# Two transformer layers on one core: longer transfer times in the list run, and a row's output projection and SwiGLU four attention steps later

## The chip, the cores and the metric

The kernel runs on one core of a Trainium2 chip. The metric is the device time of one execution in microseconds (us), given as the median of several runs.

## The reference

The input is eight sequences ("rows" below) of 512 tokens with 256 channels, and a condition vector of 64 numbers for each row. Two layers follow one another, all in float32:

```
# layer 0: conditioned norm, GELU-gated feed-forward, quantised down projection, residual
scale = cond @ norm_w.T + 1.0
h = x * (scale * rsqrt(mean(x * x) + 1e-6))
val, gate = split(h @ up_w.T, 2)              # 256 -> 2 x 1024
h = val * gelu(gate)
x = x + act_quant(h) @ weight_quant(down_w).T # 8-bit steps per token, weights of -1, 0, 1
# layer 1: adaptive norm, attention, adaptive norm, SwiGLU
n = gamma(cond) * rmsnorm(x) + beta(cond)
attn = softmax(0.25 * q k^T) v                # 16 heads of 16 channels, 512 x 512 scores each
x = x + alpha(cond) * (attn @ W_o.T)
n = gamma2(cond) * rmsnorm(x) + beta2(cond)
x = x + alpha2(cond) * ((silu(n @ gate_w.T) * (n @ hidden_w.T)) @ out_w.T + out_b)
```

## The kernel before

The kernel does not write its instructions in program order. Each piece of work is recorded with `op(engine, cost, fn, reads, writes, at, ...)`: its engine, an assumed duration, what it reads and writes, and a due time `at`. Then `Plan.order` runs a list schedule over all recorded pieces: on each engine it takes the piece with the earliest due time that could start now, by assumed durations and assumed latencies, and the instructions are issued in the order so found. Buffers are slots of named pools (`pools`), and the list run also decides which slot a value gets. On the chip each engine then executes its list strictly in that order and waits on semaphores. Nothing of the assumed times is on the chip; they decide the order alone.

Three things shape the list run beside costs and due times. `LATENCY` is the time from the end of a piece to when another engine may use it: 0.1 to 0.25 us for compute engines and 2.5 us for `SP`, which issues nearly all transfers. `lag` adds to that for single pieces. `SEEDS` holds one number for each 12 us of assumed time; a number other than 0 shifts due times of some lines in that stretch and changes how PE pieces of one kind are grouped (`nudge`).

The work falls into stages. Layer 0 of rows 0 to 5 comes first (up to about 210 us): `up_tile` makes a tile of 128 tokens with full-array matmuls (line 763), GELU on ACT (770), the gate product on DVE (797), the quantisation, a transposing transfer on SP (`qtrans`, line 840), and `down` (848). Layer 0 of rows 6 and 7 is mixed into the attention of row 0 as filler.

The attention of a row has 4 units of 4 heads (two halves `c` of the channels, two groups `j` in each), 32 units in all, and 4 steps a unit, 128 steps in all, which the list run places `STEP` = 5.8 us apart. For a unit, `load_unit` fetches q, k and kd (differences of k) from DRAM into `aq` and `ad` (line 976); `maxima` (1021) multiplies q and k to find the largest score of each query, six steps ahead (`LEAD`), which DVE reads off (1030); `shift` brings the maxima back as a row vector through a transposing transfer (1064); `scores` (1003, 1006) computes the shifted scores, ACT takes the exponential (1037), and `products` (1082) multiplies with v. There are three buffers for q and two for k. A k buffer is free again after the first step of `scores` of its unit (line 1006 with k), and the first `maxima` of the next unit but one need the new k about two steps later.

Between the steps PE does filler, mostly in 32-column quarters of the array (`quarters`, line 428): the projection of the next row (`project`, whose results `send` writes to DRAM as `hld` and `hdd`, line 890, eight transfers for k and its differences and four for q of each half), and the output projection and SwiGLU of the row before (`project_out`, `swiglu`). `gather` brings a unit's products out: to `zd` in DRAM (1096), back as sums `rec` and heads `zn` (1112, 1115), the reciprocal to `rd` (1118) and back (1123), and POOL multiplies (1127). `project_out` reads that, DVE multiplies by the condition's alpha (`gate`, 1164), and POOL adds to x (1173). `swiglu` starts with a norm (squares on DVE 601, root on POOL 611 and 613, scaling on DVE 619), POOL adds the output bias times alpha (`obs`, 1188), and then come gate and hidden products, the down product, `gate_and_add` again, and the store.

`load_gates(b)` fetches the alphas of row b into one of two `als` buffers (1134, on SP), and POOL multiplies them with the bias (1139). The buffer is that of row b - 2, and is free when the last `gate` (1164) of that row's `swiglu` is done. POOL's list is executed in order, so what stands behind line 1139 waits for that transfer too.

The loop over steps places a row's output projection and SwiGLU by due time:

```
        if w >= 1 and k == 0:
            d = s + 2.5 + 0.8 * (w - 1)
            project_out(w - 1, fill(d))
            swiglu(w - 1, fill(d), d + 2.5, fill, PACE)
```

Of the kernel before, what the change touches and what calls it, by code (L numbers as in the profile page):

```python
# [51 lines left out]
DH = 16  # L52
# [22 lines left out]
class Plan:  # L75
# [19 lines left out]
    LOOK = 12.0  # L95
    SPREAD = 1.5
    SEEDS = [
        0, 113879, 0, 0, 0, 0, 0, 0, 0, 691441, 257665, 0, 717272, 393272, 0, 554462, 316701, 670129, 416392,
        721209, 474305, 0, 537810, 342162, 308204, 358595, 0, 701966, 797240, 775750, 239774, 554473, 917419,
        473329, 441941, 90862, 278546, 410234, 995329, 846992, 293684, 929624, 744201, 712144, 709987, 445396,  # L100
        898520, 758230, 941880, 341522, 204408, 437273, 600013, 665815, 561999, 815879, 930, 731008, 247712,
        207304, 666590, 130391, 5386, 637252, 0, 357611, 936297, 455395, 157162, 681884, 543189, 851877,
        58582, 407043, 728554, 327633, 571631, 96113, 784247, 475861, 58555, 909861,
    ]

    def __init__(self, pools):
# [2 lines left out]
    def op(self, engine, cost, fn, reads=(), writes=(), at=0.0, also=(), mode="full", gate=None, mark=None, loads=False, lag=0.0):  # L109
        o = Op()  # L110
        o.loads, o.lag = loads, lag
        o.gate, o.mark = gate, mark
        o.engine, o.cost, o.fn, o.at, o.n, o.mode = engine, cost, fn, at, len(self.ops), mode
        deps = set()
        for v in reads:
            deps.update(v.writers)
            v.readers.append(o.n)
        for v in writes:
            deps.update(v.writers)
            deps.update(v.readers)  # L120
            v.writers, v.readers = [o.n], []
        deps.discard(o.n)
        o.deps = deps
        o.vals = list(dict.fromkeys([*writes, *reads, *also]))
        for v in o.vals:
            v.touch += 1
        o.users, o.waiting, o.ready, o.end = [], len(deps), 0.0, None
        for d in deps:
            self.ops[d].users.append(o.n)
        self.ops.append(o)  # L130
        return o
# [178 lines left out]
def dma(kb):  # L310
    return max(0.6, kb / 250)
# [3 lines left out]
def two_layers(ctx: ExitStack, tc: tile.TileContext, x, cond_t, cond_w, up_t, down_t, qkvo_t, gh_t, out_t, out_b, out):  # L315
# [53 lines left out]
    def mem(v):  # L369

        kind, i = v.slot[0]
        arena = {"b": banks, "4": a4, "2": a2, "q": aq, "d": ad, "al": als, "ob": obs}[kind]
        n = len(v.slot)
        return arena[:, i, :] if n == 1 else arena[:, i : i + n, :]
# [69 lines left out]
    def load(name, dst, src, at, cost=0.6, gate=None, queue=sp):  # L444
        op("SP" if queue is sp else "ACT", cost, lambda: queue.dma_start(out=dst(), in_=src), writes=[V[name]], at=at, gate=gate)

    load("ct", lambda: ct, cond_t, -89, queue=se)
    load("nw", lambda: mem(V["nw"])[:C, :D], cond_w[:, :D], -95)
    load_x(0, -96, n=2)
    wup, up_v = {}, up_t.rearrange("(c p) f -> p c f", p=P)  # L450

# [302 lines left out]
    def up_tile(b, t, ht, at, late=False):  # L754
# [94 lines left out]
                    mem(py)[:, :D], i[:, f * P : (f + 1) * P], w, start=f == 0, stop=f == NF - 1  # L849
                )  # L850

        op("SP", 1.5, qtrans, reads=[q], writes=[qt], at=a8, lag=1.0)
        op("PE", 0.9, down, reads=[qt, *wq], writes=[py], at=a14, gate=after(a14) if late else None,
           mode="columns" if late else "full")
        op(
# [19 lines left out]
    def project(b, at, places):  # L875
# [7 lines left out]
        def send(s, hl, m, a):  # L883

            for k in range(4):
                l = k % 2 if s else k // 2
                o = hdd[b % 2, c] if s == 2 else hld[b % 2, c, s]
                op(
                    "SP", dma(m / 2),
                    lambda l=l, k=k, o=o: sp.dma_start(out=o[:, k], in_=mem(hl)[:, l * m : (l + 1) * m]),  # L890
                    reads=[hl], writes=[vhld[b % 2][c][s][k]], at=a, lag=1.5,
                )

        for c in range(NC):
# [72 lines left out]
    def load_unit(m, at):  # L967


        b, c, j = units[m]  # L970
        for s, name in enumerate(("q", "k", "kd")):
            w = val[name, m] = Val(name)

            def fetch(s=s, w=w):
                i = hdd[b % 2, c] if s == 2 else hld[b % 2, c, s]
                sp.dma_start(
                    out=mem(w).bitcast(F32), in_=i[4 * j : 4 * j + 4].rearrange("(p e) k d s -> (e k d) p s", e=2)
                )

            op("SP", dma(384 if s == 2 else 512), fetch, reads=vhld[b % 2][c][s], writes=[w], at=at + 5 * (s == 2),  # L980
               lag=1.0)

    def tile_of(m, name, p, e):

# [56 lines left out]
    def shift(m):  # L1041


        k = m % 2
        at = when(4 * m - LEAD + 3 + HALF)

        def column(i):
            return thirds[:, k].rearrange("p t (e r) -> p e t r", e=2)[:, :, :, :8].rearrange(
                "p e t (i l) -> p i e t l", l=4
            )[:, :, :, :, i]  # L1050

        def whole(v):
            return v[:, k].rearrange("p (i e) t -> p i e t", e=2)

        def split():
            ve.tensor_copy(column(0), whole(tops))
            ve.tensor_tensor(whole(rest), whole(tops), column(0), op=ALU.subtract)
            ve.tensor_copy(column(1), whole(rest))
            ve.tensor_tensor(column(2), whole(rest), column(1), op=ALU.subtract)

        op("DVE", 0.95, split, reads=[vtop[k]], writes=[vthird[k]], at=at)

        def send():
            sp.dma_start_transpose(
                shifts[:, k, :].rearrange("r (t q) -> r t q", t=NT), thirds[:, k].rearrange("q t r -> q (t r)")
            )

        op("SP", 1.2, send, reads=[vthird[k]], writes=[vshift[k]], at=at, lag=1.0)

    def weigh(s):  # L1070
        n, kc = divmod(s, 4)
# [17 lines left out]
    def gather(n):  # L1089

        b, c, j = units[n]
        pa, zc = val["pa", n], Val("zc")
        at = when(4 * n + 5.1)
        op("ACT", act(512), lambda: se.activation(mem(zc), mem(pa), AF.Identity), reads=[pa], writes=[zc], at=at)
        d = vzd[b % 2][c]
        op("SP", dma(256), lambda: sp.dma_start(out=zd[b % 2, c, j], in_=mem(zc)), reads=[zc], writes=[d], at=at)
        if j == 0:
            return
        if c == 0:
            val["zn", b] = Val("zn")  # L1100
        zn, s = val["zn", b], Val("s")

        def z_of():
            return mem(zn)[:, c * S : (c + 1) * S]

        def blocks():
            return zd[b % 2, c].rearrange("j (i r) s -> (j i) r s", r=32)

        r, vr = rec[:, c, :], vrec[c]
        op(  # L1110
            "SP", 0.6,
            lambda: sp.dma_start(out=r, in_=blocks()[:, DH, :].rearrange("h (k s) -> h k s", k=DH)),
            reads=[d], writes=[vr], at=at,
        )
        op("SP", dma(256), lambda: sp.dma_start(out=z_of(), in_=blocks()[:, :DH, :]), reads=[d], writes=[zn], at=at)
        op("DVE", 0.35, lambda: ve.reciprocal(r, r), writes=[vr], at=at)
        op(
            "SP", 0.6, lambda: sp.dma_start(out=rd[b % 2, c].rearrange("h (k s) -> h k s", k=DH), in_=r),
            reads=[vr], writes=[vrd[c]], at=at,
        )  # L1120
        op(
            "SP", dma(256),
            lambda: sp.dma_start(out=mem(s), in_=rd[b % 2, c].unsqueeze(1).to_broadcast([8, DH, S])),
            reads=[vrd[c]], writes=[s], at=at,
        )
        op(
            "POOL", pool(512), lambda: gp.tensor_tensor(z_of(), z_of(), mem(s), op=ALU.mult),  # L1127
            reads=[s], writes=[zn], at=at + 2,
        )
# [149 lines left out]
    for s in range(-LEAD, 4 * len(units)):  # L1279
        w, k = divmod(s, 16)  # L1280
        m, qc = divmod(s + LEAD + 4, 4)
        if qc == 0 and 2 <= m < len(units):
            load_unit(m, when(s))
        for p in range(2):
            half_step(s, p)
        if (s + LEAD) % 4 == 3 and s + LEAD < 4 * len(units):
            shift((s + LEAD) // 4)
        if s >= 1:
            weigh(s - 1)
            if s % 4 == 0:  # L1290
                gather(s // 4 - 1)
        if w >= 0 and k == 0 and w + 1 < B:
            project(w + 1, fill(s - 1), [fill(s + d) for d in (1, 3, 6, 9, 11, 13)])
        if s == 0:
            for n in range(LATE * NT):
                b, t = B - LATE + n // NT, n % NT
                up_tile(b, t, hts[b], lambda i, n=n: fill((0.5 + 2.05 * n if n < LATE * NT - 1 else 17.5) + i), True)
        if w >= 0 and k == 8:
            load_gates(w)
        if w >= 1 and k == 0:  # L1300
            d = s + 2.5 + 0.8 * (w - 1)
            project_out(w - 1, fill(d))
            swiglu(w - 1, fill(d), d + 2.5, fill, PACE)
    weigh(4 * len(units) - 1)
# [46 lines left out]
```

## Time and profile before

| | us |
|---|---|
| median of 3 runs | 1064.88 (1060.07 to 1069.7) |
| profiled execution | 1064.92 |
| its span, first to last instruction | 1063.1 |
| PE busy in the span | 1031.8 (97%) |
| DVE busy | 636.9 (60%) |
| ACT busy | 525.9 (49%) |
| POOL busy | 219.6 (21%) |
| mean granted PE clock | 0.995 |

The profile is of one execution. An engine is busy when it executes; what it waited for before an instruction is told in brackets as "idle time and releaser". "SPq" is the queue of SP, which only issues transfers. PE's share says that it is nearly always at work; a clock below 1 says that PE was slowed for a part of the stretch.

### The profile page before, as it was taken

The numbers are of one execution on the slowest core, as the hardware profiler recorded it, in microseconds if no ns is written. First come the engines' busy times: TensorE is split into PE (matmuls) and PEld (weight loads), VectorE is DVE, ScalarE is ACT, GpSimd is POOL, SyncE is SP. The second block draws the span as 40 slices with busy tenths as digits, with TensorE's granted clock in tenths as the row PEclk, the third lists the DMA queues.
The fourth block names the chain that finished last, engine by engine and source line by source line (L and its number), as shares of the span: only waits on it lengthen the run. The fifth ranks groups of instructions, "written<-read, shape, count | busy, mean of one in ns | idle before, by whom it ended". The sixth has DMA issues, their size and how long they took to land.

```text
span 1063.1 us, 21750 instructions
## 1 busy us (share of the span) xinstructions
PE 1031.8 (97%) x9016; PEld 425.4 (40%) x9016; DVE 636.9 (60%) x1060; ACT 525.9 (49%) x722; POOL 219.6 (21%) x214
## 2 busy tenths in 40 slices
PE   7999989999999999999999999999899999999998
PEld 3445445433333333433443343334333433342446
DVE  3765546878776765576558547665676465663131
ACT  3434424357677645455546553564556355546221
POOL 2100100001000331043123212321331132223342
PEclk9999999999999999999999999999999999999999
DMA  6344683227564754475256537634752745321100
GB/s 197 88 106 104 187 209 75 50 55 199 147 161 95 201 157 134 138 221 186 83 163 205 144 116 219 190 99 134 218 158 85 198 149 147 126 80 47 33 21 20
DMA packets 131235, 142.07 MB, mean 134 GB/s; under 512 B 60472, under 2 KB 87288, under 8 KB 131136
## 3 DMA queue, kind: packets, MB, share of 16 engines
q1 hardware_dynamic: 130912, 140.42, 47.3%
q8 instruction: 70, 1.15, 0.4%
q10 hardware_dynamic: 224, 0.26, 0.1%
q14 instruction: 29, 0.24, 0.1%
HBM read 69.08 MB, written 59.00 MB: 120 GB/s over the span
## 4 chain that ended last, share of the span: by engine, by line
PE 84%; DMA 9%; DVE 2%; SPq 1%; ACT 1%; POOL 1%; issue 1%; DVEq 0%; ACTq 0%; POOLq 0%
PE banks L428 38%; PE banks L763 15%; PE banks L1082 9%; PE banks L1021 6%; PE banks L1006 6%; DMA aq<-hld 3%; PE banks L1201 3%; DMA a<-a 2%; PE banks L848 2%; PE banks L1003 1%; PE banks L1242 1%; PE banks L434 1%; DMA rd<-rec 1%; SPq L890 1%; DMA a<-rd 1%; DVE tops L1030 1%
## 5 line engine op out<-in xcount | busy, mean ns | idle before, releaser
L1030 DVE TENSOR_REDUCE tops<-banks 128x2 f32<-128x1024 f32 x256 | 308.5, 1220 | 137.7 <-PE banks L1021 135.2
L1037 ACT ACTIVATE a<-banks 128x1024 f32<-128x1024 f32 x256 | 252.5, 1024 | 128.3 <-PE banks L1006 102.8
L428 PE MATMUL banks<-a,gh 128*32 128x512 f32 x1792 | 206.1, 594 | 0.0
L763 PE MATMUL banks<-a,a 128*128 128x512 f32 x384 | 174.8, 603 | 0.6 <-ACT a L726 0.6
L1082 PE MATMUL banks<-a,vts 128*32 128x512 f32 x1024 | 135.2, 606 | 0.1
L1229 POOL TENSOR_TENSOR a<-a 128x512 f32<-128x512 f32 x64 | 81.8, 1279 | 233.8 <-ACT a L1225 223.5
L1021 PE MATMUL banks<-aq 64*128 64x512 f32 x512 | 103.0, 440 | 11.9 <-DMA aq<-hld 6.0
L428 PE MATMUL banks<-wout,a 128*32 128x256 f32 x1792 | 106.9, 381 | 0.0
L763 PEld LDWEIGHTS banks<-a,a 128*128 128x128 f32 x384 | 71.3, 192 | 81.7 <-issue 73.9
L428 PEld LDWEIGHTS banks<-a,gh 128*32 128x32 f32 x1792 | 54.0, 110 | 121.4 <-issue 111.1
L1219 DVE SCALAR_TENSOR_TENSOR a<-a,banks 128x512 f32<-128x512 f32 x64 | 43.8, 685 | 86.5 <-ACT a L1214 86.2
L770 ACT ACTIVATE a<-banks,rstds 128x512 f32<-128x512 f32 x64 | 43.5, 687 | 96.7 <-PE banks L763 87.0
L797 DVE SCALAR_TENSOR_TENSOR a<-banks,rstds,a 128x512 f32<-128x512 f32 x64 | 47.9, 749 | 72.0 <-PE banks L763 54.3
L1006 PE MATMUL banks<-aq,ad 64*128 64x512 f32 x384 | 78.5, 434 | 2.2 <-ACT a L1037 2.1
L1021 PEld LDWEIGHTS banks<-aq 64*128 64x128 f32 x512 | 45.8, 186 | 81.1 <-issue 31.9
L428 PEld LDWEIGHTS banks<-wout,a 128*32 128x32 f32 x1792 | 54.7, 110 | 51.1 <-issue 21.3
L1214 ACT ACTIVATE a<-banks 128x512 f32<-128x512 f32 x64 | 38.2, 597 | 71.2 <-PE banks L428 59.6
L1225 ACT ACTIVATE a<-banks 128x512 f32<-128x512 f32 x64 | 38.3, 598 | 61.0 <-PE banks L428 51.5
L1173 POOL TENSOR_TENSOR x<-x,a 128x512 f32<-128x512 f32 x31 | 40.5, 1309 | 107.9 <-DVE a L1164 107.9
L428 PE MATMUL banks<-a,a 128*32 128x512 f32 x512 | 58.9, 594 | 0.0
L428 PE MATMUL banks<-a,qkvo 128*32 128x512 f32 x448 | 57.4, 609 | 0.0
L428 PE MATMUL banks<-qkvo,a 128*32 128x256 f32 x896 | 55.0, 381 | 2.3 <-POOL a L1127 2.3
(110 smaller groups left out, 928.9 us busy)
## 6 DMA issues: line engine op xcount, KB each, us to landing
hld<-a SPq DMA_DIRECT2D x128, 256.0 KB
aq<-hld SPq DMA_DIRECT2D x64, 512.0 KB
hdd<-a SPq DMA_DIRECT2D x64, 192.0 KB
ad<-hdd SPq DMA_DIRECT2D x32, 384.0 KB
zd<-a SPq DMA_DIRECT2D x32, 256.0 KB
a<-zd SPq DMA_DIRECT2D x16, 256.0 KB
a<-rd SPq DMA_DIRECT2D x16, 256.0 KB
out_dram<-x SPq DMA_DIRECT2D x15, 256.0 KB
```

The costliest lines, as they stand in the source:

```text
L428: pe.matmul(o[32 * i : 32 * i + 32, :], w[:, 32 * i : 32 * i + 32], r, start=start, stop=stop)
L763: (quarters if late else pe.matmul)(mem(us[half, j]), mem(ht)[:, c * S + t * P : c * S + (t + 1) * P], mem(wup[c, 2 * half + j]), start=c ...
L770: se.activation(mem(gs[j]), mem(us[1, j]), AF.Gelu, scale=rstds[:, b, t : t + 1])
L797: lambda v=us[0, j], g=gs[j], j=j: ve.scalar_tensor_tensor(mem(h)[:, j * 512 : (j + 1) * 512], in0=mem(v), scalar=rstds[:, b, t : t + 1], ...
L1006: pe.matmul(mem(sc)[:, e, :], k, tile_of(n, "q", p, e), start=False, stop=True, skip_group_check=kc > 0,)
L1021: pe.matmul(mem(pm)[:, e, :], tile_of(m, "q", p, e)[:, qc * P : (qc + 1) * P], tile_of(m, "k", p, e), start=True, stop=True,)
L1030: lambda: ve.tensor_reduce(tops[:, m % 2, 2 * p : 2 * p + 2, qc], mem(pm), AX.X, ALU.max, negate=True),
L1037: lambda: se.activation(mem(e).rearrange("p (i s) -> p i s", i=2), mem(sc), AF.Exp, scale=0.25),
L1082: pe.matmul(mem(pa)[32 * i : 32 * i + 32, :], vts[:, b % 2, kc, h : h + 32], mem(es[i // 2])[:, (i % 2) * S : (i % 2 + 1) * S], start=kc = ...
L1173: lambda: gp.tensor_tensor(xs, xs, mem(w).rearrange("p (t d) -> p t d", t=2), op=ALU.add),
L1219: lambda t=t, i=ps[0]: ve.scalar_tensor_tensor(mem(t), in0=mem(t), scalar=1.0, in1=mem(i), op0=ALU.add, op1=ALU.mult),
L1229: "POOL", pool(512), lambda t=t, h=hid, g=gt: gp.tensor_tensor(mem(g), mem(t), mem(h), op=ALU.mult),
```

## The change

The change touches what the list run assumes and one due time; no instruction is added or taken away, but the order on every engine, and the slots, are found anew.

- The `lag` of transfers grows: the transposing transfers of quantised tiles 1 to 2 us, the sends of q, k and differences 1.5 to 5, the fetches of q, k and kd 1 to 3, the transposing transfers of the maxima 1 to 3, the transfers in `gather` from 0 to 1 or 1.5. The load of the alphas (`load_gates`) keeps none.
- `d`, the due step of the output projection and SwiGLU of row w - 1, goes from s + 2.5 + 0.8 (w - 1) to s + 6.5 + 0.5 (w - 1).
- The first, small load of condition weights (`nw`) is issued by ACT instead of SP.
- `SEEDS` is another list (81 numbers instead of 82).

```
     SEEDS = [
-        0, 113879, 0, 0, 0, 0, 0, 0, 0, 691441, 257665, 0, 717272, 393272, 0, 554462, 316701, 670129, 416392,
...
+        209955, 113879, 0, 0, 0, 0, 0, 240022, 14449, 948552, 209771, 801933, 0, 859222, 0, 991400, 636493,
...
     ]
     load("ct", lambda: ct, cond_t, -89, queue=se)
-    load("nw", lambda: mem(V["nw"])[:C, :D], cond_w[:, :D], -95)
+    load("nw", lambda: mem(V["nw"])[:C, :D], cond_w[:, :D], -95, queue=se)
     load_x(0, -96, n=2)
...
-        op("SP", 1.5, qtrans, reads=[q], writes=[qt], at=a8, lag=1.0)
+        op("SP", 1.5, qtrans, reads=[q], writes=[qt], at=a8, lag=2.0)
...
-                    reads=[hl], writes=[vhld[b % 2][c][s][k]], at=a, lag=1.5,
+                    reads=[hl], writes=[vhld[b % 2][c][s][k]], at=a, lag=5.0,
...
             op("SP", dma(384 if s == 2 else 512), fetch, reads=vhld[b % 2][c][s], writes=[w], at=at + 5 * (s == 2),
-               lag=1.0)
+               lag=3.0)
...
-        op("SP", 1.2, send, reads=[vthird[k]], writes=[vshift[k]], at=at, lag=1.0)
+        op("SP", 1.2, send, reads=[vthird[k]], writes=[vshift[k]], at=at, lag=3.0)
...
-        op("SP", dma(256), lambda: sp.dma_start(out=zd[b % 2, c, j], in_=mem(zc)), reads=[zc], writes=[d], at=at)
+        op("SP", dma(256), lambda: sp.dma_start(out=zd[b % 2, c, j], in_=mem(zc)), reads=[zc], writes=[d], at=at, lag=1.5)
...
-            reads=[d], writes=[vr], at=at,
+            reads=[d], writes=[vr], at=at, lag=1.0,
...
-        op("SP", dma(256), lambda: sp.dma_start(out=z_of(), in_=blocks()[:, :DH, :]), reads=[d], writes=[zn], at=at)
+        op("SP", dma(256), lambda: sp.dma_start(out=z_of(), in_=blocks()[:, :DH, :]), reads=[d], writes=[zn], at=at, lag=1.5)
...
-            reads=[vr], writes=[vrd[c]], at=at,
+            reads=[vr], writes=[vrd[c]], at=at, lag=1.0,
...
-            reads=[vrd[c]], writes=[s], at=at,
+            reads=[vrd[c]], writes=[s], at=at, lag=1.5,
...
         if w >= 1 and k == 0:
-            d = s + 2.5 + 0.8 * (w - 1)
+            d = s + 6.5 + 0.5 * (w - 1)
             project_out(w - 1, fill(d))
             swiglu(w - 1, fill(d), d + 2.5, fill, PACE)
```

## The prediction

> **What bounds the kernel now.** I read the totals first.
>
> ```profile
> span 1063.1 us, 21750 instructions
> PE 1031.8 (97%) x9016; PEld 425.4 (40%) x9016; DVE 636.9 (60%) x1060; ACT 525.9 (49%) x722; POOL 219.6 (21%) x214
> ```
>
> PE sets the end. The matmuls stay the same ones, so only PE's waits, and work done at a lower clock, can move the time. The waits of PE come next (engine, line, releaser; total, times, longest).
>
> ```profile
> PE banks L1021 <- DMA aq<-hld: 6.0, 4, 3.6
> PE banks L1021 <- DVE tops L1030: 5.6, 7, 2.4
> PE banks L434 <- DMA x<-in_x_dram: 5.3, 2, 3.8
> PE banks L848 <- DMA a<-a: 3.7, 2, 2.3
> PE banks L428 <- POOL a L1127: 2.3, 2, 1.3
> PE banks L1006 <- ACT a L1037: 2.1, 4, 0.9
> ```
>
> With the small rows behind them these are some 27 us. Third, the windows of 8 us around the longer waits (length, busy time of PE, PEld, DVE, ACT, POOL, then granted clock, DMA share, GB/s).
>
> ```profile
> 656.00:664.00 8.00, 6.99 (x44) 2.36 (x48) 3.49 (x7) 3.80 (x5) 2.73 (x4) 0.79 0.84 229
> 764.00:772.00 8.00, 7.06 (x58) 2.42 (x60) 4.12 (x6) 3.06 (x5) 2.58 (x2) 0.79 0.52 180
> 852.00:860.00 8.00, 7.87 (x72) 3.32 (x76) 4.36 (x5) 3.81 (x4) 2.53 (x3) 0.79 0.20 68
> 957.00:965.00 8.00, 7.39 (x66) 2.49 (x68) 5.35 (x15) 6.77 (x9) 3.83 (x4) 1.00 0.28 76
> ```
>
> A mean of 0.79 over 8 us is 0.21 x 8 / 0.5 = 3.4 us at half clock. It follows waits of 1.67, 2.43 and 3.56 us; the wait of 0.87 us before the last window did not bring it. What it costs is seen in PE's own rows:
>
> ```profile
> 852.13 0.50 PE L1021 MATMUL banks<-aq 64*128 64x512 f32 x2 [3.56 <-DMA aq<-hld]
> ...
> 853.25 1.94 PE L1082 MATMUL banks<-a,vts 128*32 128x512 f32 x8
> ...
> 859.45 1.07 PE L1082 MATMUL banks<-a,vts 128*32 128x512 f32 x8
> ```
>
> Eight products take 1.94 us there and 1.07 us six us later. 3.4 us at half clock are at most 1.7 us lost; group by group against the usual distance from one start to the next I find 1.5 us for each of the three. A long wait so costs its length and 1.5 us more. The Trainium skill ("TensorE: Matmul & The Clock Gate", Part 1) lets the clock fall to half after an idle window of about 3.4 us. The trace differs: 1.67 us of idle was followed by it too. By the rule alone only the 3.56 us wait would carry the extra 1.5 us.
>
> **The k loads (PE L1021 waiting for aq<-hld), -8.0.** The four waits are 0.32, 0.45, 1.67 and 3.56 us, 6.0 together. A k buffer is free after its last scores at line 1006; the fetch (976) then stands in SP's queue behind what the list run put there. SP before the wait of 1.67 us:
>
> ```profile
> 642.26 3.62 SPq L890 DMA_DIRECT2D hld<-a  x4
> 645.98 3.92 SPq L890 DMA_DIRECT2D hdd<-a  x3
> 649.99 0.93 SPq L976 DMA_DIRECT2D aq<-hld  x1
> ```
>
> Each send holds SP for about 0.9 us. In all four waits three to seven sends stand just ahead of the fetch. I call cover the PE work between the freeing scores and the first maxima that read the new k: the four had 8.1, 7.0, 6.5 and 6.2 us, and needed cover plus wait, 8.4 to 9.8. Fetches without sends ahead managed with 6.2 to 7.9 and no wait. In the changed order, with the same durations, covers are 7.9 or more without sends and 8.6, 8.8, 8.8, 9.0, 10.3, 10.4 with them. So the waits go, and the half clock after two of them: -(6.0 + 2 x 1.5) = -9.0; I keep back 1.0, since needs reach 9.8 and four covers lie below it. Ends: -5 (each of the four short by up to 1.2) and -9.
>
> **project_out and swiglu four steps later, -2.3.** For a row that moves 8 groups of output products on PE, two gates on DVE (1164) and two adds on POOL (1173), and then the whole SwiGLU: squares, root, scalings and 16 transposes of the norm, two bias adds, its gate, hidden and down groups, 16 ACT, 8 DVE and 8 POOL instructions, two gates, two adds, two stores on SP. PE waited for POOL's line 1127 at 359.17 (1.31 us) and 455.63 (1.04 us), the total of 2.3 above, with 21.3 and 21.6 us of cover from the last products; the smallest cover becomes 29.8. That chain is two round trips through DRAM and POOL's multiply; one late by 8 us more would still be hidden. Row 7's own cover grows from 16.5 to 21.6 and had no wait. Ends: -2.3 and 0.
>
> **Transposed quantised tiles (848 <- DMA a<-a), -2.0.** The waits of 1.42 us at 146.00 and 2.33 us at 155.40 followed covers of 12.2 and 7.9 us, in a stretch (140 to 158) where the transfers' share was 0.85. Covers of the tiles in that stretch become 12.8, 11.8, 16.3 and 9.5; the needs were 13.6 and 10.2. Some 0.8 to 1.8 of the 3.7 us stays: -2.0, ends -3.7 and 0.
>
> **The load of the alphas (als), +3.2.** This is what the move is paid with. POOL executes in order. Its line 1139 waits for als, which is fetched only when the last gate (1164) of the row two before has freed the buffer, and these gates now come later, while line 1139 gets no lag. Row 7 shows the chain:
>
> ```profile
> 948.08 1.28 POOL L1173 TENSOR_TENSOR x<-x,a 128x512 f32<-128x512 f32 x1 [11.87 <-DVE a L1164]
> 952.15 0.73 POOL L1139 TENSOR_TENSOR obs<-ob,als 128x256 f32<-128x256 f32 x1 [2.79 <-DMA als<-ald]
> 952.84 2.52 POOL L1173 TENSOR_TENSOR x<-x,a 128x512 f32<-128x512 f32 x2
> ```
>
> The fetch is issued at 947.96, line 1139 starts 4.2 us later. Queued behind it on POOL are the adds 1173; the squares of the norm (601) on DVE wait for those, the maxima's reduction (1030) stands behind the squares, and PE's line 1021 waits for that reduction: 10.55 us from PE's last wout group (946.64) to line 1021 (957.19), of which the work put between covers 9.9; PE waits 0.87. At 764.94 the same chain through the root and the scaling (619) gave the 2.43 us wait and a half clock. So before: 2.43 + 1.5 + 0.87 = 4.8 us. From issue to line 1139 it took 3.4 to 7.4 us over the rows. Covers before, rows 0 to 7: 61, 19.9, 18.2, 18.4, 15.4, 10.6, 11.7, 9.9. After: 56.1, 13.1, 11.1, 12.1, 10.7, 9.4, 10.5, 14.5. Five rows (2 to 6) are where only two or three were. With the median fetch of 6.0 us the chain is 10.55 + 1.9 = 12.4 long and the five come short by 1.3, 0.3, 1.7, 3.0 and 1.9; but the chain needs DVE's squares to stand right ahead of a reduction, which was so in two of the three tight rows. Two thirds of 8.2 is 5.5, with 1.5 for the clock in about two: 8, so +3.2. Ends: -3.8 (1 us remains, the squares fall behind the reductions) and +19 (below).
>
> **Condition weights on ACT's queue, start, +0.4.** ACT now issues them ahead of its other loads, SP one less (its issue took 0.57 us). PE takes both halves of the x transposes together and the small product 516 ahead of them. The first up matmul, at 8.84, then waits for DVE's constants (1.02 us) ahead of the copy: about 9.25. The x halves' own waits (5.3 us) stay. Ends -0.7 and +1.5. The Trainium skill ("DMA: Bandwidth & Descriptors", Issuing engines are not separate DMA queues) says that another issuing engine saves only the time of issuing; the 0.57 us would be all.
>
> **The rest, -1 and 0.** 436 switches between matmul forms on PE become 438; by the usual distances of neighbouring groups the order's work is 1022.1 before and 1020.8 after: -1. ACT swaps its function table 18 times for 16 (1.28 us each, ACT at 49%; cover is the scores ahead of it), against which fewer scores have the short covers (up to 1.3 us) of the 2.1 us row: 0, ends -2 and +2.6. The last 40 us are the same.
>
> Sum: -8.0 - 2.3 - 2.0 + 3.2 + 0.4 - 1.0 = -9.7. The profiled execution took 1064.92 (span and 1.8 around it), as the median, 1064.88. Forecast: 1064.9 - 9.7 = **1055.2 us**.
>
> **Rivals.**
>
> *The alphas' wait takes the place of all that is removed (slower).* If every fetch takes the slowest 7.4 us, the chain is 13.8 long, the five rows wait 2.7, 1.7, 3.1, 4.4, 3.3 (15.2) and row 1 another 0.7, each of the five with a half clock: 16 + 7.5 = 23.5 instead of 4.8, +18.7, or 1070.7. It decides from about 6.4 us a fetch upwards if the clock drops each time. For it: fetches of 6.5, 6.6 and 7.4 occurred. Against it: the last three were 5.1, 3.4 and 4.1, and DVE, 60% busy, may take other work first.
>
> *The alphas' wait does not come.* Squares stand behind reductions or later, 1 us remains, and the transposes' waits go whole: -9.7 - 7.0 - 1.7 = about -18, 1046.5. For it: rows 1 to 5 before, with chains of the same make, had a single long wait. Against it: covers fall in seven rows of eight.
>
> *Given back in short waits.* The k loads and project_out save 12.3 us with the clock; if PE, sooner at its next maxima, waits half of it for DVE's reductions (5.6 us in seven waits now) the sum is -9.7 + 6.1, 1061. For it: 1030 is the costliest group of DVE. Against it: at 60% DVE has room.
>
> That the change does nothing is excluded: the lists of all five engines differ.
>
> **How the numbers follow.** Forecast (1050 to 1060) 0.50, gain without the alphas' wait 0.20, short waits 0.17, slower rival 0.13. One per cent, about what a measurement of this kernel can tell, is 1054.2 and 1075.5. Faster: 0.21 of the forecast's 0.50, 0.20 and 0.02, so 0.43. Slower: 0.08 of the slower rival's and 0.01, so 0.09. Same: 0.48. The range, 1045 to 1070, ends just past the one rival and just short of the other, half of each beyond it.
>
> **What would show it.** Right: L1021 <- DMA aq<-hld at 1 us or less and no half clock after k; L428 <- POOL L1127 gone; L848 at 1 to 2 us; L1021 (or 1082) waiting for DVE some 10 us after the last wout products of rows 2 to 6, POOL's 1139 having waited for als just before; PE's first full-array matmul near 9.3. Wrong: k waits that remain behind sends (the needs grew with the queue), new waits of PE on lines that have none now, or half clock in more than three stretches.

## The result, and the profile after

| us | before | after |
|---|---|---|
| median | 1063.59 (1060.07 to 1069.7, 6 runs) | 1052.51 (1050.82 to 1053.49, 6 runs) |
| ratio | | 0.9889, 95% interval 0.986 to 0.9917 |
| profiled execution, its span | 1064.92, 1063.1 | 1052.31, 1050.5 |

The changed kernel is 11.1 us faster by the medians and 12.6 us by the spans of the two profiles. One execution of the run with later alphas, below, took 3606.86 us and is left out of that run's median. The totals of the page after, in the same form as before:

```profile
span 1050.5 us, 21789 instructions
PE 1029.5 (98%) x9016; PEld 425.3 (40%) x9016; DVE 644.4 (61%) x1060; ACT 524.9 (50%) x724; POOL 220.0 (21%) x214
```

The waits of PE after (engine, line, releaser; total, times, longest):

```profile
PE banks L516 <- DMA ct<-in_cond_t_dram: 8.2, 1, 8.2
PE banks L1006 <- ACT a L1037: 1.9, 2, 1.7
PE banks L428 <- DVE tops L1030: 1.7, 3, 0.9
PE banks L428 <- DMA a<-a: 1.5, 1, 1.5
PE banks L1003 <- DVE tops L1030: 1.4, 2, 1.0
```

Three rows that stood in the list before are gone: line 1021 for aq<-hld (6.0), line 848 for the transposed tiles (3.7) and line 428 for POOL's line 1127 (2.3). Line 1021 waits for DVE's reductions only once, 0.2 us, where it was 5.6. The first row is new, and it is the start; before, the start's waits stood under lines 434 and 516, 5.9 together. The rows of 1.5 (line 428, a transposed tile) and 1.7 and 1.4 (reductions) are new as well. PE there, after:

```profile
8.20 0.56 PE L516 MATMUL banks<-ct,a 64*128 64x8 f32 x2 [8.20 <-DMA ct<-in_cond_t_dram]
...
10.94 3.78 PE L763 MATMUL banks<-a,a 128*128 128x512 f32 x4 [0.39 <-DVE a L728]
```

The first up matmul starts at 10.94 us; before it was 8.84. ACT's queue shows what PE waited for:

```profile
0.72 0.55 ACTq L445 DMA_DIRECT2D a<-in_cond_w_dram  x1
...
1.94 0.49 ACTq L445 DMA_DIRECT2D ct<-in_cond_t_dram  x1
```

The condition vectors, 2 KB, are the last of three transfers, issued at 1.94 instead of 0.72, and line 516 waits for them until 8.20.

Between the start and the end the clock fell once, not three times. A window (length, busy time of PE, PEld, DVE, ACT, POOL, clock, DMA share, GB/s) and the wait ahead of it:

```profile
335.40 0.51 PE L1006 MATMUL banks<-aq,ad 64*128 64x512 f32 x2 [1.71 <-ACT a L1037]
```

```profile
336.00:344.00 8.00, 8.00 (x50) 2.09 (x52) 4.74 (x8) 5.20 (x7) 0.00 (x0) 0.79 0.40 98
```

PE is busy for all of these 8 us, and yet 3.4 us of them ran at half clock: a busy share of 100% hides this loss, and only the clock's column shows it.

### The profile page after: what moved, and what is told of

Same layout as the page of the kernel before. It is cut to its first block, busy times and chain, and to the rows that moved or that the text cites. A ratio compares the mean times of both kernels' runs of the same rounds, so it can differ in the third digit from the quotient of the medians.

```text
span 1050.5 us, 21789 instructions
## 1 busy us (share of the span) xinstructions
PE 1029.5 (98%) x9016; PEld 425.3 (40%) x9016; DVE 644.4 (61%) x1060; ACT 524.9 (50%) x724; POOL 220.0 (21%) x214
## 4 chain that ended last, share of the span: by engine, by line
PE 90%; DVE 3%; issue 2%; DMA 1%; POOL 1%; ACT 1%; ACTq 0%; DVEq 0%; POOLq 0%
PE banks L428 42%; PE banks L763 16%; PE banks L1082 9%; PE banks L1021 7%; PE banks L1006 6%; PE banks L1201 3%; PE banks L848 2%; PE banks L1003 1%; PE banks L1242 1%; PE banks L434 1%; DVE tops L1030 1%; DVE a L619 1%; DMA als<-ald 1%; PE banks L901 1%; DVE a L601 1%
## 5 line engine op out<-in xcount | busy, mean ns | idle before, releaser
L1037 ACT ACTIVATE a<-banks 128x1024 f32<-128x1024 f32 x256 | 251.8, 1023 | 136.7 <-PE banks L1006 109.4
L1006 PE MATMUL banks<-aq,ad 64*128 64x512 f32 x384 | 76.3, 427 | 1.9 <-ACT a L1037 1.9
L1006 PEld LDWEIGHTS banks<-aq,ad 64*128 64x128 f32 x384 | 35.0, 185 | 50.6 <-issue 24.7
```

The costliest lines, as they stand in the source:

```text
L1006: pe.matmul(mem(sc)[:, e, :], k, tile_of(n, "q", p, e), start=False, stop=True, skip_group_check=kc > 0,)
L1037: lambda: se.activation(mem(e).rearrange("p (i s) -> p i s", i=2), mem(sc), AF.Exp, scale=0.25),
```

## The experiments

Most experiments leave the list run as it is and edit its result: `emitted = plan.order()` is changed, and the loop issues `emitted`. So single instructions move and all others keep their place, which a new list run would not grant. `named(o, ...)` tells an SP piece by the function that made it; `clash(a, b)` is true if two pieces depend on one another or share a buffer. The runs below were made in three groups, each on another chip; each run is compared with runs of the kernel before in its own group, whose medians were 1061.49, 1064.67 and 1065.02 us. Since before's own executions scatter by 9 to 15 us within a group, two variants of the changed kernel are compared by their medians (their executions scatter by 2 to 4 us, by 8 with the later alphas) and by their traces, and not by their ratios to before. The changed kernel itself was run in the group of the result alone.

### Sends behind the k fetches, in the order of before

```
    for f in [o for o in emitted if named(o, "load_unit") and o.vals[0] in [val["k", m] for m in (11, 15, 19, 27)]]:
        p = emitted.index(f)
        back = [i for i in range(p) if emitted[i].engine == "SP"][-7:]
        for i in back[::-1]:
            o = emitted[i]
            if named(o, "project") and not named(o, "project_out") and not any(clash(o, emitted[q]) for q in range(i + 1, emitted.index(f) + 1)):
                emitted.remove(o)
                emitted.insert(emitted.index(f) + 1, o)
```

Expected:

> The order of before, but on SP the four k fetches that made PE wait (the last unit of rows 2, 3, 4 and 6) are issued ahead of the sends that stood directly in front of them; PE, ACT, DVE and POOL keep their lists. Theory (the sends in front make the fetch late): the four waits, 6.0 us, fall to under 1, at most one stretch of half clock stays, the time falls by 7 to 9 us to about 1055.5. Rival (the cover is too short for any fetch): the waits keep 4 us or more and the gain is under 2. Rival (the delayed sends come late themselves): the waits go, new ones of line 1021 or of ACT's and DVE's writes into the buffers of the sends take their place, gain 2 to 5.

Measured: 1077.37 us (ratio 1.016, 1.0119 to 1.0201), slower by 16 us. The profile is of the fastest of its four executions, 1072.97 us, and is 8 us longer than that of before. The largest row of PE's waits in it:

```profile
PE banks L1003 <- DMA shifts<-thirds: 11.3, 4, 7.1
```

There is no row for aq<-hld any more, with the same lists on PE, ACT, DVE and POOL: the sends in front of the fetch made it late, not a cover too short for any fetch. Of the third expectation the kind came (new waits in place of the old), but not the place, line 1003 instead of 1021, and not the gain of 2 to 5 us. SP around the fetch for row 4:

```profile
645.48 1.23 SPq L1064 DMA_TRANSPOSE shifts<-thirds  x1
654.10 0.36 SPq L976 DMA_DIRECT2D aq<-hld  x1
654.57 3.89 SPq L890 DMA_DIRECT2D hld<-a  x4
658.55 4.70 SPq L890 DMA_DIRECT2D hdd<-a  x4
...
666.49 1.40 SPq L1064 DMA_TRANSPOSE shifts<-thirds  x1
```

SP issued nothing from 646.7 to 654.1, since the fetch at the head of its queue waited for its buffer. The eight sends came after it, and the transposing transfer of the maxima (1064) stood behind those; line 1003 waited 7.1 us for it at 671.78. What the changed order does is another thing: its k fetches with sends in front have more PE work between the freeing scores and the maxima, 8.6 us and more by the prediction's covers.

### The alphas earlier, in the order of before and of after

A third buffer; the fetch, line 1134, moves up.

```
-    als = const.tile([P, 2, 2 * D], F32, name="als")
+    als = const.tile([P, 3, 2 * D], F32, name="als")
...
+    for b in range(B):
+        val["al", b].slot = (("al", b % 3),)
+        f = next(o for o in emitted if named(o, "load_gates") and val["al", b] in o.vals)
+        p = q = emitted.index(f)
+        while emitted[q].end > f.end - 30 and not clash(f, emitted[q - 1]):
+            q -= 1
+        emitted.insert(q, emitted.pop(p))
```

Expected, on before:

> The order of before, with a third buffer for the alphas and line 1134 issued some 10 us earlier; nothing else moves. Theory of the prediction (the waits at 764.94 and 957.19 belong to the chain through the alphas): both go, with one stretch of half clock, gain 4.8 us. Rival (at both places the last gate or DVE's own work is nearly as late): half of the two waits or more stays, gain under 2.5 us.

and on after:

> The changed order, with a third buffer for the alphas, so that line 1134 can be issued some 10 us earlier; nothing else moves. Theory (the chain through the alphas now costs PE only the 1.02 us before line 1003 at 377.37 and a few tenths): that wait goes, line 1139 waits nowhere for als, gain 1.0 to 1.7 us. Rival by the working of the prediction (the chain costs 8 us): gain 5 to 8 us. Rival (the second gate and the square behind it are late by themselves): gain 0.

The issue came earlier than the "some 10 us" of both texts: 24 to 36 us before line 1139 starts, in all rows. On before, the time was 1055.84 against 1064.67 in its group (ratio 0.9938, 0.9905 to 0.997), 3 to 10 us faster, 6.6 by the middle of the ratio; the waits of 2.43 and 0.87 us for DVE are not in the trace any more (0.3 is left at the second place), and their half clock is gone. So 4.8 us was a fair price, but not all of the 6.6 is the alphas': in this profile, which is of the slowest of ten executions, the waits for k loads are 4.3 us instead of 6.0, and 2.6 us of waits are new (0.95 for line 1164, 0.91 for a transfer of the maxima, 0.7 for ACT). On after it was 1049.35 us (ratio 0.9895, 0.9866 to 0.9923) against 1052.51 for the changed kernel itself, 3.2 less, and 2.8 less than the run with ct first below; only the second comparison is within a group. By the two profiles the spans differ by 3.3, of which 0.6 is the start, where ct happened to land earlier (first up matmul 10.32 instead of 10.94): the alphas cost the changed kernel 2.7 us. The wait of 1.02 us at 377.37 is gone, and so is that of 0.29 at 668.66. That is neither the 8 us of the prediction nor nothing, and more than the 1.0 to 1.7 us of the first theory: the waits of PE alone account for some 1.7 us.

### The alphas later, in the order of after

```
    for b in range(2, 7):
        f = next(o for o in emitted if named(o, "load_gates") and val["al", b] in o.vals)
        p = emitted.index(f)
        q = next(i for i in range(p, len(emitted)) if named(emitted[i], "swiglu", "store"))
        ...
        emitted.insert(q, emitted.pop(p))
```

> The changed order, but in rows 2 to 6 the fetch of the alphas (1134) is issued behind the next store on SP, some 2 us later; nothing else moves. By the working of the prediction (chain of 6.4 us plus the fetch, against covers of 11.1, 12.1, 10.7, 9.4, 10.5) the five rows come short by 2.6, 1.7, 2.6, 3.3 and 1.1 us, and with half clock behind most of them the time grows by 10 to 17 us. Rival (DVE's own second gate comes about as late as the alphas, and PE has other work in front of the line that waits): under 3 us.

Measured: 1062.11 us (median of nine), ratio 1.0013 to before (0.9991 to 1.0034): 9.9 us above the run with ct first, which is in the same group, and 9.6 above the changed kernel itself. The whole gain is gone. POOL's line 1139 in rows 3 and 6 (start, length, then idle time and releaser), first after, then this run:

```profile
567.96 0.73 POOL L1139 TENSOR_TENSOR obs<-ob,als 128x256 f32<-128x256 f32 x1 [0.97 <-DMA als<-ald]
...
856.29 0.73 POOL L1139 TENSOR_TENSOR obs<-ob,als 128x256 f32<-128x256 f32 x1 [1.89 <-DMA als<-ald]
```

```profile
569.11 0.73 POOL L1139 TENSOR_TENSOR obs<-ob,als 128x256 f32<-128x256 f32 x1 [3.01 <-DMA als<-ald]
...
863.43 0.73 POOL L1139 TENSOR_TENSOR obs<-ob,als 128x256 f32<-128x256 f32 x1 [6.39 <-DMA als<-ald]
```

POOL waits 2.0 us longer in row 3 and 4.5 in row 6. The waits of PE that answer:

```profile
PE banks L1021 <- DVE tops L1030: 5.9, 3, 4.1
...
PE banks L1021 <- DVE a L926: 1.6, 1, 1.6
```

Line 1021 now waits 1.63 us (row 3), 1.57 (row 4) and 4.12 (row 6), the last two with half clock behind them. So the chain that the prediction named is there. It is weaker than by its working: three of the five rows wait, 7.3 us in all instead of 11.3, and two have half clock behind them. In rows 3, 4 and 6 nearly all of POOL's longer wait (2.0, 1.3 and 4.5 us) reaches PE; in rows 2 and 5 POOL waits 1.1 and 1.2 us longer and PE does not wait. So on this chain the changed kernel has less than half a us of slack in rows 3 and 6, none in row 4, and at least 1 us in rows 2 and 5.

### The start

First, ct ahead of the other loads on ACT's queue, in the order of after:

```
+    first = next(o for o in emitted if o.engine == "ACT" and V["ct"] in o.vals)
+    emitted.remove(first)
+    emitted.insert(0, first)
```

> The changed order, but ACT issues the condition vectors ct first, then the condition weights, then the piece of the up weights (in the change ct comes last of the three); no other instruction moves. Theory (ct lands late because it stands third in ACT's queue): line 516 starts near 5 us instead of 8.2, the first up matmul near 8.9 instead of 10.9, and the time falls by 2 us, to about 1050.5. Rival (the start waits for the second half of x or the first up weights, which share the transfer engines): the first up matmul stays at 10.4 or later, gain under 0.5 us.

Measured: 1052.19 us, no difference from 1052.51 that these runs can tell; span 1049.8. Line 516 starts at 7.27 and the first up matmul at 10.00. The releaser is now another:

```profile
7.27 0.56 PE L516 MATMUL banks<-ct,a 64*128 64x8 f32 x2 [7.27 <-DMA a<-in_cond_w_dram]
```

The theory missed. Of the rival the gain by the medians came (0.3 us), but not its late matmul, and the start waits for the condition weights, which neither named. ct's place is worth at most the 0.9 us; the rest is the condition weights themselves, which on ACT's queue, issued at 1.30, land about 2 us later than before from SP's, issued at 1.25 (line 516 started at 5.08). Second, the weights go back to SP, between the halves of x, together with the earlier alphas:

```
+    w = next(o for o in emitted if o.engine == "ACT" and V["nw"] in o.vals)
+    w.fn = lambda: sp.dma_start(out=mem(V["nw"])[:C, :D], in_=cond_w[:, :D])
+    emitted.remove(w)
+    emitted.insert(1 + next(i for i, o in enumerate(emitted) if o.engine == "SP"), w)
```

> The changed order with two edits after the list run: a third buffer for the alphas with line 1134 issued 24 to 35 us before line 1139 starts, and the first condition weights issued by SP between the two halves of x, as before the change; ACT issues ct first of its two loads. Theory (in the change the condition weights and ct land late on ACT's queue behind and beside the up weights): line 516 starts at 5 to 6 us instead of 7.3 to 8.2, the first up matmul at 9.0 to 9.5 instead of 10.0 to 10.9, and with the 2.7 us from the alphas the time is 1047 to 1048.5. Rival (line 516 ahead of the transposes, or the second half of x, sets the start): the first up matmul stays at 10 or later, 1049 to 1050.

```profile
5.87 0.56 PE L516 MATMUL banks<-ct,a 64*128 64x8 f32 x2 [5.87 <-DMA a<-in_cond_w_dram]
...
8.60 4.63 PE L763 MATMUL banks<-a,a 128*128 128x512 f32 x5 [0.39 <-DVE a L728]
```

(ACT issued the up weights first and ct second here, at 1.18.) The start is as expected and better, 8.60, 2.3 us ahead of the changed kernel's. Line 516 ahead of the transposes does no harm. The time is 1049.55 us, ratio 0.9863 (0.9838 to 0.9889), not the 1047 to 1048.5 but in the rival's 1049 to 1050, though the start is not the rival's. It is the same time as with earlier alphas alone, 1049.35, in another group. In this profile a wait at 370.34 took 2.12 us with half clock behind it, where the run with early alphas alone had 1.67 us without, and one at 688.82 took 1.42 us that the other did not have. Together some 3 us, they cost more than the 1.7 us that the start gained against that run. They are hardly a matter of the single execution: the granted clock was 0.996 or 0.997 in all four executions here, and 0.998 in three of the four with early alphas alone. Why the earlier start should bring them stays open.

### What belongs to the settings, and what to the seeds

A new list run with a part of the change finds another order altogether, so these runs tell of classes of waits, not of single ones. Without seeds (`SEEDS = []`): the kernel before; the longer times alone; the later due time alone.

> The kernel before with an empty list of seeds (no due time is shifted in the list run): the base of four runs without seeds. More and longer waits of PE than before, time 1070 to 1110. Waits of PE for k loads and for line 1127 are expected again (5 us or more together).

> As the run without seeds, plus the longer times for transfers alone. Theory (the lags take away the waits for k loads and transposed tiles): these rows of PE's waits fall by 70% or more against the run without seeds, and the time by 5 to 15 us. Rival (the gain lies in the seeds that were found anew for the change): the waits fall by less than half or others take their place, time within 3 us of the run without seeds or above it.

> As the run without seeds, plus the output projection and SwiGLU four steps later alone. Theory (the move takes away only the waits for line 1127): that row goes, 1 to 4 us, the k loads keep waiting. Rival (the later gates make the alphas late): waits of line 1021 for DVE grow by 3 us or more and the time does not fall.

Measured: 1112.55 (just above its range), 1116.93 and 1101.98 us. So without seeds the longer times alone gain nothing, and the later due time alone is 10.6 us faster, more than its theory's 1 to 4; all its executions (1100.44 to 1105.21) lie below those of the base (1106.34 to 1120.36). A run put down for both parts together was by mistake the kernel without seeds and without either part once more, so its expectation does not apply; it repeats the first, 1107.11 us. Both parts together without seeds was not measured.

> Without seeds, the longer times for transfers and the later output projection and SwiGLU together (the condition weights stay on SP). If the two parts help each other without seeds: under 1099, below both parts alone (1117 and 1102) and below neither (1112). If the order without seeds is simply luck of the draw for PE's waits for DVE: between 1100 and 1118, with no waits for transfers after the start and 20 us or more of waits for DVE and ACT.

Waits of PE without seeds, first with no part of the change, then with the longer times (line numbers are 7 lower here; 1014 is 1021, 1023 is 1030, 421 is 428, 841 is 848, 1120 is 1127):

```profile
PE banks L1014 <- DVE tops L1023: 6.8, 9, 1.2
...
PE banks L841 <- DMA a<-a: 3.3, 1, 3.3
...
PE banks L421 <- POOL a L1120: 1.8, 1, 1.8
```

```profile
PE banks L1014 <- DVE tops L1023: 13.1, 18, 1.6
PE banks L644 <- DVE a L612: 5.9, 2, 5.1
```

With the longer times no wait for a transfer or for line 1127 is left after the start. The time does not fall; waits for DVE take their place, and the mean clock is 0.977 instead of 0.986. With the later due time alone the row for line 1127 is gone too, while line 841 waits 4.0 us and line 1014 has a new wait of 3.0 us for DVE's line 1212 (1219).

Waits for k loads, expected in the base and in the third run, did not come in any of these. They are not in the run of the old kernel with new seeds below either. So that the longer times remove them is not shown: of the orders made with the old times, only that of before has them (and its edited copy with the earlier alphas). For the transposed tiles and the maxima's transfers (841 and 996, that is 848 and 1003) it is different: each of the other orders with the old times waits for them, 3.8 to 5.8 us in all, and no order with the longer times does, on these lines. Last, the lists of seeds exchanged:

> The changed kernel with the list of seeds of before: every other part of the change. Theory (the lags, the later due time and the queue carry the gain): below 1064, waits for transfers gone. Rival (seeds fit only the due times and lags that they were found with): 1085 to 1120, waits for transfers gone, waits for DVE and ACT 20 us or more and more stretches of half clock.

> The kernel before with the list of seeds of the changed kernel, nothing else. Theory (the seeds carry the gain by themselves): below 1064. Rival (seeds fit only the due times and lags that they were found with): 1085 to 1120, with waits for transfers again beside those for DVE and ACT.

Measured: the changed kernel with the old seeds 1101.13 us, the kernel before with the new seeds 1136.19. Both rivals came, the second with 1136 above its bound; it waits for transfers again (2.8 at line 428, 2.5 at 1003, 1.3 at 848). With the old seeds the changed kernel waits for no transfer after the start either, and the waits of PE are these:

```profile
PE banks L1021 <- DVE tops L1030: 10.0, 15, 1.0
PE banks L1006 <- ACT a L1037: 8.3, 11, 2.4
PE banks L1003 <- DVE tops L1030: 7.0, 9, 1.5
```

The waits are only half of what seeds made for another order cost. The span of the changed kernel with the old seeds is 49.0 us longer, 1099.5 instead of 1050.5. PE's waits grow by 23 us, and PE's busy time grows by 25.1, from 1029.5 to 1054.6. The mean clock of 0.991 instead of 0.998 is some 16 us more at half clock, at most 8 us lost. The rest, some 17 us, goes with 482 switches between matmul forms (rows x columns of the array) instead of 440, counted in the traces; the seeds also change how PE's pieces are grouped. What a switch costs was not measured, so this part is argued.

So the 11 us cannot be shared out between lags, due time and seeds: the later due time gained 10.6 us in an order without seeds, the longer times gained nothing there, and no order without the seeds made for it comes below 1100. What can be told is which waits are gone, and that new seeds were needed to keep DVE's and ACT's waits, half clock and form switches down.

## Why the prediction was right or wrong

The forecast was 1055.2 us, the range 1045 to 1070; 1052.5 is inside, and "faster" held. But two terms failed. They erred in opposite directions, so it is in part luck that the sum came within 3 us. By PE's waits, and 1.5 us for each stretch of half clock:

| term | predicted | measured |
|---|---|---|
| k loads | -8.0 | -9.0: all four waits and both half clocks gone |
| project_out (1127) | -2.3 | -2.3: gone |
| transposed tiles | -2.0 | -2.2: 3.7 gone, 1.5 at 372.08 for a late tile |
| alphas | +3.2 | -2 to -3.3 |
| start | +0.4 | +2.1 |
| scores and ACT | 0 | +1.2: 0.3 less waiting, one half clock more |
| order of the forms | -1 | not measured apart |

*The alphas* were the step with the wrong sign. The chain was right, and it is the place where this change can be lost: the fetch issued later cost 9.9 us, just under the 10 to 17 by its working. The size was wrong by its first number. The prediction took 6.0 us from issue to line 1139, the median of before; after, rows 2 to 6 took 5.3, 5.4, 4.9, 4.3 and 3.2 (the issue times of line 1134 against the starts of line 1139). With those the same working has the five rows short by 0.6, 0, 0.6, 1.3 and 0, 2.5 us in all. The 2.7 us that the third buffer saved agrees in the sum, but by chance: rows 2 to 6 show one wait of PE behind this chain, 0.29 us in row 4, and 1.0 of the 2.7 was row 1, where the fetch stood behind a transposing transfer of 3.63 us on SP. So the working asks too much of those rows even with the shorter fetch. Before, the chain cost 4.8 us, so the term was about -2, or -3.3 by the waits alone (1.5 us of those after belong to it). That the fetch became quicker because fewer sends stand ahead of it in rows 3 to 6 is argued from SP's list, not tried. If so, one part of the change shortened the transfer that the other part put under pressure, and the prediction priced it from the old rows.

*The start* lay outside its ends (-0.7 to +1.5). The prediction saw that PE would take line 516 first, and counted 0.4 for DVE's constants. It treated the landing of the condition weights and of ct as unmoved. It is these that moved: weights from SP at 1.25 were there at 5.08, from ACT at 1.30 at 7.27 (the run with ct first), and ct, third on ACT's queue, at 7.59 to 8.20. In the changed kernel itself the weights were issued at 0.72, and PE's rows do not show when they landed. The Trainium skill ("DMA: Bandwidth & Descriptors", Issuing engines are not separate DMA queues) says that transfers of all issuing engines run on the same 16 DMA engines and interleave. The trace fits that, as far as it goes: ACT's queue was no faster way, 2.1 us were lost, not the 0.57 of issuing saved. Why a transfer issued at the same time lands 2 us later is not shown; with the weights on ACT, SP issues both halves of x and the up weights earlier (1.75 instead of 2.49), and that these are ahead of it is argued only.

*The k loads and project_out* came as worked out, within 1 us. Covers of 8.6 us and more with sends in front were enough, and the 1.0 that was kept back was not needed. (The needs before were misread: cover plus wait of the four are 7.5 to 9.8 by the prediction's own numbers, not 8.4 to 9.8.) That the sends are the cause, the run with the sends behind the fetches shows; that the longer times move them, no run shows.

*The tiles* came out by luck: the 1 to 2 us that were to stay at line 848 are gone, and a wait of 1.51 us on a line that had none, 428 at 372.08, takes their place in the sum.

*The rival in which short waits give the gain back* did not come with the new seeds (waits for DVE other than the alphas' are about 3 us in both); something like it is seen without them and with the old ones, in orders that differ throughout. (The saving of the k loads and project_out that this rival halves is 11.3 us by its terms, 9.0 and 2.3, and not 12.3; the rival's time hardly moves.) The rival in which the alphas' wait does not come, 1046.5, was nearer than the forecast in its mechanism. The start, the 2.7 us that the alphas still cost, the tile's wait and the half clock behind line 1006 kept the time from it.

Of the signs named for being right, the k loads and line 1127 came. The full-array matmul near 9.3 (10.94), line 848 at 1 to 2 us (0) and the waits for DVE behind the wout products of rows 2 to 6 (0.29) did not.

The measured terms add to -12.2 with -2 for the alphas, and to -13.5 with -3.3. The last matmul starts at 1046.2 instead of 1059.2, 13.0 us earlier.

## What to carry to other kernels

When a change moves work and loosens a queue at once, price the moved step's transfers by the queue as it will be, not by the median of the old one (here 3.2 to 5.4 us instead of 6.0). A fetch brought to the head of an in-order queue before its buffer is free holds everything behind it: here 6 us of waits went and 11 of another kind came. A first load's queue is part of the critical path: look at what else is issued in the first 8 us before moving it, and at when it lands. A list run with other assumptions is another order: compare its waits, its clock and its form switches before giving a gain to one setting.

## What the runs showed of the hardware that was not expected

- The length of a wait alone does not decide whether the clock falls. Over the eight profiles of before, after and their edited orders, waits up to 1.51 us were never followed by half clock and those from 2.4 us always; in between both occurred. The same wait of 1.71 us for line 1037 near 335 was followed by 3.4 us at half clock in four profiles and by none in a fifth (the run with the later alphas); a wait of 2.33 us at 155.40 before the change was not followed by any, one of 1.57 us at 670.44 in that fifth run was. The Trainium skill ("TensorE: Matmul & The Clock Gate", Part 1) calls the window of about 3.4 us free-running, that is, not begun by the wait. That part agrees with one wait having both outcomes; that a whole window must be idle does not, since waits of half its length brought the fall.
- Short waits close together bring the fall too, in the orders whose seeds do not fit. The changed kernel with the old seeds, PE's waits and then the window:

```profile
366.72 0.49 PE L1021 MATMUL banks<-aq 64*128 64x512 f32 x2 [1.00 <-DVE tops L1030]
368.44 0.39 PE L1003 MATMUL banks<-shifts,pick 64*128 64x512 bf16 x2 [1.23 <-DVE tops L1030]
```

```profile
366.00:382.00 16.00, 13.53 (x110) 5.19 (x114) 10.49 (x12) 8.77 (x10) 1.03 (x2) 0.79 0.74 195
```

  That is 6.7 us at half clock (0.21 x 16 / 0.5) behind two waits of at most 1.23 us. So a list of the longest waits does not find every loss of clock; the clock's column does.
- The time at half clock came in multiples of 3.4 us: 3.4 in most stretches; by the windows of 8 us, 6.7 us around a wait of 3.10 (845.94, the order of before with early alphas) and 10.2 around the one of 7.12 (the sends behind the fetches).
- The kernel before varies more from run to run than the changed one: 1060.07 to 1069.7 against 1050.82 to 1053.49 in six runs each. Its waits for transfers are what the changed order no longer has; that these make the spread was not tried by itself. The granted clock goes with it: over all its executions, from 1.0 in one of 1056.08 us to 0.991 in one of 1072.6. By this clock at most 0.009 x 1070.8 = 9.6 of these 16.5 us are lost work.
